# Expert weights split by ScalarE and token rows turned by VectorE in an adaLN block with mixture of experts

## The chip, the core and the metric

The kernel runs on one core of a Trainium2 chip. A core has TensorE (PE; its weight loads are shown apart as PEld), VectorE (DVE), ScalarE (ACT), GpSimd (POOL) and SyncE (SP), each with an instruction queue of its own that is worked off in order, and 16 DMA engines that they share. The metric is the device time of one execution in microseconds, as the median of several runs. The profiled execution is one of its own; its span, from the first instruction to the last, is what the profile's rows add up in.

## The reference

32 sequences of 256 tokens with 128 features each (8192 tokens) pass through one transformer block in float32. Cut to what matters:

```python
mod = (silu(c) @ wmod).reshape(32, 6, 1, 128)          # shift, scale, gate for both halves
h = layernorm(x) * (1 + ca) + sa
x = x + ga * attention(h)                              # 16 heads of 64, causal, softmax over the queries
h = layernorm(x) * (1 + cb) + sb
scores = sigmoid(h @ gate_weight.T);  sc = scores + gate_bias
# 32 experts in 4 groups of 8: the best 2 groups of a token, in them its best 6 experts
tw = scores[topidx] / (sum + 1e-20) * 0.2
routed = sum_e cw[e] * ((silu(h @ w_gate[e]) * (h @ w_up[e])) @ w_down[e])       # 64 wide each
shared = (silu(h @ sh_gate) * (h @ sh_up)) @ sh_down                             # 64 wide
anchor = the same with one of 16 pairs, 32 wide, that of the best expert         # times 0.1
x = x + gb * (routed + shared + anchor)
```

Two facts matter below. A token visits exactly two of the four groups. And the weight of an expert is a factor per token, so it can be multiplied onto the hidden activations before the down product.

## The kernel before

Tokens are handled in 16 chunks of 512 (`CH`); 128 partitions hold four tokens each (`NT` is 4). The order of the instructions on every engine is the order in which the Python code issues them (`manual_schedule`); a table of portions with due steps (`deal`) places the layer norms and the routing between the matmuls.

**Attention** (up to about 884 us) runs over 16 x 8 pairs of heads. Beside it each chunk is normalised a second time, and its rows, 128 features (`D`) followed by 4 x 13 routing numbers (`NG` groups of `GW`), are put into the tile `rows`. The features are turned by a way through DRAM: `through_dram` writes them (`hd`), `load_blocks` reads them back in four DMAs so that each 32 x 32 block lies where a VectorE stream transpose (`norm2_turn`) makes the whole matrix of it. The routing numbers of a group are its eight expert weights, the weights of its four anchor pairs, and the row of the result that the token is to be written to; `route_write` puts the weights in with GpSimd. `route_send` then scatters every row twice, once to each of its token's groups, into the DRAM tensor `rows_d`, where the tokens of one group stand together. `late_loads` loads the down weights `wd_sb` and `ad_sb` at attention step 9 (`s == NP + 1`).

**The expert part** works through 35 tiles (`LISTS`) of 512 rows of one group. Which group and which rows a tile has is computed on the chip (`Tiles`), so SP reads two words of a table per tile and uses them in addresses. A tile has five up products `k` (four of the 8 x 64 expert columns, 128 at a time, `KU` is 4, and one of the 4 x 32 anchor columns); `up(j, k)` multiplies the turned rows `h` with gate and up weights into PSUM, ScalarE applies Silu, VectorE multiplies with the up product and then with the tokens' weights `bt`. `down(j, k)` multiplies that with the down weights into `py`, and stands on TensorE behind the next `up`. `send` copies `py` and scatters the rows with four GpSimd DMAs into `y_d`, one row for each (token, group).

What a tile needs is prepared during earlier tiles, from the loop at L1403:

- `fetch_rows(j + 3)` and `fetch_weights(j + 2)` at k = 0. Rows come as one DMA of 128 partitions x 4 whole rows; gate and up weights as four.
- `weights_mine(j + 2)` at k = 1: VectorE masks the routing numbers of all four groups by the tile's own group and sums over the groups. The table `mine` for that is made in `Tiles`.
- `weights_turn(j + 2)` at k = 2: TensorE transposes the weights, ScalarE copies them out of PSUM (`cwt`), SP writes them to DRAM (`cd`) and reads them back spread over the partitions (`bt`) in six DMAs. Partition 64 q + i of product k holds expert 2 k + q's hidden unit i, so each k has weights of its own in `bt`.
- `rows_turn(j + 1)` at k = 3: four TensorE transposes of the rows, one ScalarE copy to `h`.

**The closing pass.** Once both results of all tokens of a chunk are written, from tile 17 on, `pass_load` reads them (`s`, two tiles) and the gate at k = 4. `pass_sum` at k = 3 of the next tile adds both and the shared result on VectorE and multiplies by the gate on GpSimd; `pass_out` at k = 1 of the tile after it adds the residual and stores. Between attention and the tiles stand seven pairs of the shared expert (`shared_up`, `shared_down`), beside which the first tiles are prepared.

All DMAs of this part except the scatters are issued by SP, in program order.

Of the kernel before, what the change touches and what calls it, by code (L numbers as in the profile page):

```python
# [50 lines left out]
ROW = D + NG * GW  # L51
# [5 lines left out]
def adaln_block_kernel(  # L57
# [80 lines left out]
    def late_loads():  # L138

        nc.sync.dma_start(out=wd_sb, in_=w_down.rearrange("(k p) m -> p k m", p=P))  # L140
        nc.sync.dma_start(out=ad_sb, in_=an_down.rearrange("(k p) m -> p k m", p=P))
        nc.sync.dma_start(out=sg_sb, in_=sh_gate)
        nc.sync.dma_start(out=su_sb, in_=sh_up)
        for h in range(P // SI):
            nc.sync.dma_start(out=sd_sb[h * SI : (h + 1) * SI], in_=sh_down)
# [174 lines left out]
    with ExitStack() as actx:  # L320
# [325 lines left out]
        def norm2_modulate(c):  # L646
            rows = rowp.tile([P, NT, ROW], F32, tag="rows", name=f"rows_{c}")
            modulated(rows[:, :, 0:D], chunk[c].pop("xh"), chunk[c].pop("mb2"))
            chunk[c]["rows"] = rows
# [124 lines left out]
        def route_place(c):  # L774
# [17 lines left out]
                chunk[c]["rows"][:, :, D:].rearrange("p i (g w) -> p i g w", w=GW)[:, :, :, GW - 1],  # L792
# [44 lines left out]
        def route_write(c):  # L837

            w, ws, one = (chunk[c].pop(k) for k in ("w", "ws", "one"))
            meta = chunk[c]["rows"][:, :, D:].rearrange("p i (g w) -> p i g w", w=GW)  # L840
            wk = w.rearrange("p i (g k q) -> p i g k q", g=NG, q=2)
            for q in range(2):
                nc.gpsimd.tensor_tensor(
                    meta[:, :, :, q * EPG // 2 : (q + 1) * EPG // 2], wk[:, :, :, :, q],
                    ws.unsqueeze(2).unsqueeze(3).to_broadcast([P, NT, NG, EPG // 2]), ALU.mult,
                )
# [118 lines left out]
        class Tiles:  # L965


            def __init__(self, n, segments, name):
# [4 lines left out]
                self.mine = k_([n, NG], f"{name}_mine")  # L973

            def steps(self):
# [54 lines left out]
                def g():  # L1030
                    nc.vector.tensor_copy(self.table, self.where)

                    nc.vector.tensor_tensor(
                        self.mine,
                        self.where[:, 0, :].unsqueeze(2).to_broadcast([P, n, NG]),
                        tile_no[:, 0:NG, 0].unsqueeze(1).to_broadcast([P, n, NG]),
                        ALU.is_equal,
                    )
# [109 lines left out]
        yp = actx.enter_context(tc.tile_pool(name="y", bufs=3, reuse_waits="tile"))  # L1148
        fin = actx.enter_context(tc.tile_pool(name="fin", bufs=3, reuse_waits="tile"))
# [9 lines left out]
        def fetch_rows(j):  # L1159
# [4 lines left out]
            t["rw"] = rwp.tile([P, NT, ROW], F32, tag="rw", name=f"rw_{j}")  # L1164
            got = nc.sync.dma_start(
                out=t["rw"],
                in_=rows_d[bass.ds(r, CH), :].rearrange("(p i) f -> p i f", i=NT),
            )
            if j < FIRST:
                tc.declare_no_dep(  # L1170
                    got.ins, group="late rows", reason="this tile holds rows of earlier chunks"
                )
                tc.add_to_no_dep_group("first tiles", got.ins)

        def fetch_weights(j):
            t = T[j]
            g = t.pop("g_sp")
            for key, src, srca in (("wg", w_gate, an_gate), ("wu", w_up, an_up)):
                w = wp.tile([P, KU + 1, P], F32, tag=key, name=f"{key}_{j}")
                nc.sync.dma_start(  # L1180
                    out=w[:, 0:KU, :].rearrange("p k f -> p (k f)"),
                    in_=src[:, bass.ds(g * (KU * P), KU * P)],
                )
                nc.sync.dma_start(out=w[:, KU, :], in_=srca[:, bass.ds(g * P, P)])
                t[key] = w

        def weights_mine(j):

            t = T[j]
            of, n = t["of"]  # L1190
            mm = mp.tile([P, NT, NG, GW], F32, tag="mm", name=f"mm_{j}", bufs=1)
            nc.vector.tensor_tensor(
                mm,
                t["rw"][:, :, D:].rearrange("p i (g w) -> p i g w", w=GW),
                of.mine[:, n, :].unsqueeze(1).unsqueeze(3).to_broadcast([P, NT, NG, GW]),
                ALU.mult,
            )
            m = mp.tile([P, GW, NT], F32, tag="m", name=f"m_{j}")
            nc.vector.tensor_reduce(m, mm.rearrange("p i g w -> p w i g"), AX.X, ALU.add)
            ix = mp.tile([P, NT], U32, tag="ix", name=f"iy_{j}", bufs=5)  # L1200
            nc.vector.tensor_copy(ix, m[:, GW - 1, :])
            t.update(m=m, ix=ix)

        def weights_turn(j):
            t = T[j]
            m = t.pop("m")
            pc = ps_mm.tile([(GW - 1) * NT, P], F32, tag="mm", name=f"pc_{j}")
            nc.tensor.transpose(
                pc, m[:, 0 : GW - 1, :].rearrange("p w i -> p (w i)"), ident
            )  # L1210
            cwt = mp.tile([(GW - 1) * NT, P], F32, tag="cwt", name=f"cwt_{j}", bufs=2)
            nc.scalar.copy(cwt, pc)
            cd = cwd.tile([GW - 1, CH], F32, tag="cd", name=f"cd_{j}")
            nc.sync.dma_start(out=cd.rearrange("w (i p) -> (w i) p", p=P), in_=cwt)
            bt = bcp.tile([P, KU + 1, CH], F32, tag="bt", name=f"bt_{j}")
            for q in range(2):
# [286 lines left out]
```

## Time and profile before

| | |
|---|---|
| Median of 3 runs | 1422.85 us (1421.65 to 1423.9) |
| Profiled execution, time | 1432.95 us |
| Profiled execution, span | 1431.2 us |
| Attention, from the start to the first shared product | about 884 us |
| Expert tiles, first up product to last down product | 911 to 1411 us |
| TensorE busy | 1355.9 us (95%) |
| VectorE busy | 1039.5 us (73%) |
| ScalarE busy | 796.8 us (56%) |
| GpSimd busy | 763.7 us (53%) |
| DMA packets, bytes | 183599, 182.5 MB |
| of them under 512 B | 81520 |

Busy time is the sum of an engine's instructions and says nothing of what waits for what. The costliest groups of the expert part, from the page (line, engine, operation, result and operands with shapes, count; then busy us and mean ns of one; then idle time before them and what ended most of it):

```profile
L1246 DVE TENSOR_TENSOR a<-a,pu 128x512 f32<-128x512 f32 x175 | 120.1, 686 | 149.2 <-PE pu L1243 107.1
L1245 ACT ACTIVATE a<-pg 128x512 f32<-128x512 f32 x175 | 104.5, 597 | 181.3 <-PE pg L1242 117.7
L1242 PE MATMUL pg<-h,wg 128*128 128x512 f32 x350 | 180.7, 598 | 2.1 <-ACT h L1235 2.1
L1243 PE MATMUL pu<-h,wu 128*128 128x512 f32 x350 | 179.6, 595 | 0.0
L1268 PE MATMUL py<-wd_sb,a 128*128 x1120 | 148.1, 275 | 2.3 <-DVE a L1247 2.3
```

VectorE and ScalarE mostly wait for TensorE's products; TensorE hardly waits at all. A float32 product stands there as two records, so 175 products are 350.

### The profile page before, as it was taken

What the parts mean: (1) busy time and instruction counts of PE and PEld (TensorE: products, weight loads), DVE (VectorE), ACT (ScalarE), POOL (GpSimd) and SP (SyncE); (2) the same over time, 40 slices, a digit from 0 to 9 for tenths busy, and PEclk for the clock granted to TensorE, in tenths of its full rate; (3) what the DMA queues carried; (4) which work ended last, traced back from release to release, by engine and by line L of the source; (5) the groups of instructions that cost most, each with busy time, mean ns of one, the idle gap of its engine ahead of it and who ended that gap; (6) DMA issues with size and microseconds to landing.
All of it is one profiled execution on the core that took longest, in us unless ns stands there. A gap on an engine that the chain in (4) does not pass through costs nothing. (4 is left out here: it accounts for less than half of the span.)

```text
span 1431.2 us, 33682 instructions
## 1 busy us (share of the span) xinstructions
PE 1355.9 (95%) x10543; PEld 841.2 (59%) x10543; DVE 1039.5 (73%) x4277; ACT 796.8 (56%) x2767; POOL 763.7 (53%) x1294
## 2 busy tenths in 40 slices
PE   6999999999999999999999997889999999999994
PEld 2566565565565565565565664455666666656662
DVE  5666878878878878888878775666755667766664
ACT  3777677777777776777777774322333333332331
POOL 3536467767767767767767546335232233434333
PEclk9999999999999999999999999999999999999997
DMA  4773622022022022022131013676677787888782
GB/s 151 273 264 106 217 73 59 32 74 60 31 74 60 30 73 59 32 74 54 36 73 46 30 44 104 163 205 177 172 197 194 190 221 212 241 246 244 233 211 68
DMA packets 183599, 182.50 MB, mean 128 GB/s; under 512 B 81520, under 2 KB 142656, under 8 KB 178944
## 3 DMA queue, kind: packets, MB, share of 16 engines
q1 hardware_dynamic: 172112, 159.62, 40.3%
q0 software_dynamic: 10624, 20.21, 4.2%
q8 instruction: 86, 1.41, 0.4%
q14 instruction: 89, 0.73, 0.2%
q10 hardware_dynamic: 688, 0.53, 0.1%
HBM read 121.37 MB, written 59.70 MB: 127 GB/s over the span
## 5 line engine op out<-in xcount | busy, mean ns | idle before, releaser
L549 ACT ACTIVATE e<-e,mn 128x256 f32<-128x256 f32 (+1 forms) x1024 | 453.5, 445 | 216.9 <-DVE mn L539 186.5
L539 DVE CUSTOM_DVE_ANT_0 e<-psc,mask 128x256 f32<-128x256 f32 (+1 forms) x1024 | 305.5, 345 | 5.9 <-PE pq L468 1.4
L568 POOL TENSOR_TENSOR vs<-v,rc 128x256 f32<-128x256 f32 x256 | 151.6, 613 | 239.6 <-DVE rc L557 230.8
L1279 POOL DMA_INDIRECT y_d<-y,iy x140 | 138.0, 985 | 237.0 <-ACT y L1276 204.7
L518 PEld LDWEIGHTS psc<-q,k 64*128 64x128 f32 x2048 | 166.2, 187 | 113.4 <-issue 101.6
L1246 DVE TENSOR_TENSOR a<-a,pu 128x512 f32<-128x512 f32 x175 | 120.1, 686 | 149.2 <-PE pu L1243 107.1
L1245 ACT ACTIVATE a<-pg 128x512 f32<-128x512 f32 x175 | 104.5, 597 | 181.3 <-PE pg L1242 117.7
L518 PE MATMUL psc<-q,k 64*128 64x256 f32 (+1 forms) x2048 | 202.1, 336 | 0.0
L586 PE MATMUL pav<-e,vs 128*64 128x256 f32 (+1 forms) x2048 | 195.7, 333 | 6.3 <-POOL vs L568 3.9
L549 ACT ACTIVATION_READ_ACCUMULATOR e<-e,mn 128x1 f32 x1024 | 192.9, 188 | 0.0
L1268 PEld LDWEIGHTS py<-wd_sb,a 128*128 128x128 f32 x1120 | 146.5, 191 | 71.0 <-issue 53.0
L1242 PE MATMUL pg<-h,wg 128*128 128x512 f32 x350 | 180.7, 598 | 2.1 <-ACT h L1235 2.1
L1243 PE MATMUL pu<-h,wu 128*128 128x512 f32 x350 | 179.6, 595 | 0.0
L468 PEld LDWEIGHTS po<-wo_sb,z 128*64 128x64 f32 x2048 | 121.2, 138 | 70.2 <-issue 69.7
L586 PEld LDWEIGHTS pav<-e,vs 128*64 128x64 f32 x2048 | 127.3, 137 | 59.4 <-POOL vs L568 7.0
L479 DVE TENSOR_TENSOR v<-pv,bv_sb 128x512 f32<-128x512 f32 x128 | 88.3, 690 | 89.9 <-PE pv L468 63.5
L1268 PE MATMUL py<-wd_sb,a 128*128 x1120 | 148.1, 275 | 2.3 <-DVE a L1247 2.3
L856 POOL DMA_INDIRECT rows_d<-rows,ix x128 | 130.2, 1017 | 37.2 <-issue 34.5
L468 PE MATMUL pv<-wqkv_sb,n_t 128*64 128x512 f32 x512 | 133.3, 601 | 15.8 <-DVE q L489 15.6
L489 DVE TENSOR_SCALAR q<-pq,negbq 128x512 f32<-128x512 f32 x128 | 95.9, 750 | 60.3 <-PE pq L468 58.4
L468 PE MATMUL po<-wo_sb,z 128*64 128x128 f32 x2048 | 134.1, 274 | 0.0
L468 PE MATMUL pq<-n_t,wqkv_sb 128*64 128x512 f32 x512 | 133.4, 600 | 0.7 <-ACT n_t L302 0.7
(239 smaller groups left out, 1797.5 us busy)
## 6 DMA issues: line engine op xcount, KB each, us to landing
bt<-cd SPq DMA_DIRECT2D x70, 512.0 KB
rows_d<-blank SPq DMA_DIRECT2D x69, 360.0 KB
rw<-rows_d SPq DMA_DIRECT2D x35, 360.0 KB
wg<-in_w_gate_dram SPq DMA_DIRECT2D x35, 256.0 KB
wu<-in_w_up_dram SPq DMA_DIRECT2D x35, 256.0 KB
bt<-cd SPq DMA_DIRECT2D x140, 64.0 KB
s<-y_d SPq DMA_DIRECT2D x32, 256.0 KB
mb<-mod_dram SPq DMA_DIRECT2D x31, 256.0 KB
```

The lines of the kernel that those rows point to most:

```text
L468: nc.tensor.matmul(ps[r], a[:, r], b, start=start, stop=stop)
L518: nc.tensor.matmul(pb[h][:, cols], k[r, o + kb * P : o + (kb + 1) * P], q[r, o + kb * P : o + S], start=True, stop=True,)
L539: nc.vector.tensor_tensor_reduce(e[:, cols], ps[:, cols], mask[:, cols], 1.0, 3e38, ALU.add, ALU.min, mn[:, b, kb, h : h + 1],)
L549: nc.scalar.activation(e[:, cols], e[:, cols], AF.Exp, bias=mn[:, b, kb, h : h + 1], scale=-1.0, accum_out=sm[:, b, kb, h : h + 1],)
L568: nc.gpsimd.tensor_tensor(vs[:, 2 * b : 2 * b + 2], vt[:, 2 * b : 2 * b + 2, col : col + P].rearrange("p k (h d) -> p k h d", h=2), rc[:, ...
L586: nc.tensor.matmul(pav[h * DH : (h + 1) * DH, o + kb * P : o + S], vs[:, 2 * b + kb, h, :], e[:, 0 : 2 * P] if kb == 0 else e[:, 2 * P : 3 ...
L856: sent = nc.gpsimd.indirect_dma_start(out=rows_d[:, :], out_offset=bass.IndirectOffsetOnAxis(ap=ix[:, k, i : i + 1], axis=0), in_=rows[:, ...
L1242: nc.tensor.matmul(pg, t["wg"][:, k, :], t["h"], start=True, stop=True)
L1243: nc.tensor.matmul(pu, t["wu"][:, k, :], t["h"], start=True, stop=True)
L1246: nc.vector.tensor_mul(a, a, pu)
L1268: nc.tensor.matmul(t["py"][:, i, :], a[:, i * P : (i + 1) * P], w, start=k == 0 and i == 0, stop=k == KU and i == NT - 1,)
L1279: sent = nc.gpsimd.indirect_dma_start(out=y_d[:, :], out_offset=bass.IndirectOffsetOnAxis(ap=ix[:, i : i + 1], axis=0), in_=y[:, i, :], in ...
```

## The change

Six things change together.

1. Hidden units are dealt to partitions by turns: in product k, partition 8 i + e holds unit 16 k + i of expert e. The four expert products then share one set of spread weights, and `bt` shrinks from five slices to two. The gate and up weights, loaded as before into raw tiles, are rearranged by two ScalarE copies each (`split_weights`, for the next tile at k = 2 and 3); the down weights are rearranged by their load, in 20 DMAs instead of two.
2. Rows are read twice: 16 columns (`OWN`) that start at the tile's own group's routing numbers, and the 128 features as four DMAs of `load_blocks`. A row grows from 180 to 183 numbers so that 16 columns can be read for the last group too; GpSimd clears the added ones.
3. `weights_mine` and the table `mine` go.
4. The tokens' weights and the rows are turned by VectorE stream transposes instead of TensorE. The turned weights are written to `cd` in eight DMAs and spread by two.
5. `pass_sum` moves from k = 3 of the next tile to k = 0 of the one after it, `pass_out` from k = 1 to k = 4 of that tile. The tiles `s` come from a pool of their own with six buffers instead of the four of `xin`.
6. `route_write` writes an expert group's weights with one GpSimd multiply instead of two.

```diff
+OWN = 16
+ROW = D + (NG - 1) * GW + OWN
...
     def late_loads():
-        nc.sync.dma_start(out=wd_sb, in_=w_down.rearrange("(k p) m -> p k m", p=P))
-        nc.sync.dma_start(out=ad_sb, in_=an_down.rearrange("(k p) m -> p k m", p=P))
+        for g in range(NG):
+            wd_g = w_down[g * EPG * EI : (g + 1) * EPG * EI].rearrange(
+                "(e k i) m -> k i e m", e=EPG, i=P // EPG
+            )
+            for k in range(NE // NG):
+                nc.sync.dma_start(out=wd_sb[:, g * (NE // NG) + k, :], in_=wd_g[k])
+            nc.sync.dma_start(
+                out=ad_sb[:, g, :],
+                in_=an_down[g * P : (g + 1) * P].rearrange("(l i) m -> i l m", i=LI),
+            )
...
             rows = rowp.tile([P, NT, ROW], F32, tag="rows", name=f"rows_{c}")
+            nc.gpsimd.memset(rows[:, :, D + NG * GW :], 0.0)
...
         def fetch_rows(j):
-            t["rw"] = rwp.tile([P, NT, ROW], F32, tag="rw", name=f"rw_{j}")
-            got = nc.sync.dma_start(
-                out=t["rw"],
-                in_=rows_d[bass.ds(r, CH), :].rearrange("(p i) f -> p i f", i=NT),
-            )
+            t["rw"] = rwp.tile([P, NT, OWN], F32, tag="rw", name=f"rw_{j}")
+            t["rh"] = rwp.tile([P, CH // BLK, BLK], F32, tag="rh", name=f"rh_{j}")
+            rows = rows_d[bass.ds(r, CH), :]
+            got = [
+                nc.sync.dma_start(
+                    out=t["rw"],
+                    in_=rows_d[bass.ds(r, CH), bass.ds(t["g_sp"] * GW + D, OWN)].rearrange(
+                        "(i p) f -> p i f", p=P
+                    ),
+                ),
+                *load_blocks(t["rh"], rows),
+            ]
...
+        def split_weights(j, key):
+            t = T[j]
+            raw = t[key]
+            w = wp.tile([P, KU + 1, P], F32, tag=key, name=f"{key}_{j}", bufs=2)
+            nc.scalar.copy(
+                w[:, 0:KU, :].rearrange("p k (i e) -> p k i e", e=EPG),
+                raw[:, 0 : KU * P].rearrange("p (e k i) -> p k i e", e=EPG, k=KU),
+            )
+            nc.scalar.copy(
+                w[:, KU, :].rearrange("p (i l) -> p i l", l=NG),
+                raw[:, KU * P :].rearrange("p (l i) -> p i l", l=NG),
+            )
+            t[key] = [w[:, k, :] for k in range(KU + 1)]
...
         def weights_turn(j):
-            pc = ps_mm.tile([(GW - 1) * NT, P], F32, tag="mm", name=f"pc_{j}")
-            nc.tensor.transpose(
-                pc, m[:, 0 : GW - 1, :].rearrange("p w i -> p (w i)"), ident
-            )
-            cwt = mp.tile([(GW - 1) * NT, P], F32, tag="cwt", name=f"cwt_{j}", bufs=2)
-            nc.scalar.copy(cwt, pc)
-            cd = cwd.tile([GW - 1, CH], F32, tag="cd", name=f"cd_{j}")
-            nc.sync.dma_start(out=cd.rearrange("w (i p) -> (w i) p", p=P), in_=cwt)
-            bt = bcp.tile([P, KU + 1, CH], F32, tag="bt", name=f"bt_{j}")
+            nc.vector.tensor_copy(t["ix"], rw[:, :, GW - 1])
+            m = mp.tile([P, 2, BLK], F32, tag="m", name=f"m_{j}", bufs=2)
+            nc.vector.transpose(m.rearrange("p a c -> p (a c)"), rw.rearrange("p i w -> p (i w)"))
+            cd = cwd.tile([OWN, CH], F32, tag="cd", name=f"cd_{j}")
+            to = cd.rearrange("w (a i b c) -> a b i w c", a=2, i=2, c=BLK)
+            for a in range(2):
+                for b in range(P // BLK):
+                    nc.sync.dma_start(out=to[a, b], in_=m[b * BLK : (b + 1) * BLK, a, :])
+            bt = bcp.tile([P, 2, CH], F32, tag="bt", name=f"bt_{j}")
+            for n, part in enumerate((cd[0:EPG], cd[EPG : GW - 1])):
+                of = part.shape[0]
+                nc.sync.dma_start(
+                    out=bt[:, n, :], in_=part.unsqueeze(0).to_broadcast([P // of, of, CH])
+                )
...
         def rows_turn(j):
-            ph = ps_mm.tile([P, CH], F32, tag="mm", name=f"ph_{j}")
-            for i in range(NT):
-                nc.tensor.transpose(ph[:, i * P : (i + 1) * P], rw[:, i, 0:D], ident)
             t["h"] = mp.tile([P, CH], F32, tag="h", name=f"h_{j}", bufs=2)
-            nc.scalar.copy(t["h"], ph)
+            nc.vector.transpose(t["h"], t.pop("rh").rearrange("p x r -> p (x r)"))
...
-            nc.vector.tensor_mul(a, a, t["bt"][:, k, :])
+            nc.vector.tensor_mul(a, a, t["bt"][:, k // KU, :])
...
-                if k == 1 and j + 2 < LISTS:
-                    weights_mine(j + 2)
                 if k == 2 and j + 2 < LISTS:
                     weights_turn(j + 2)
+                if k in (2, 3) and j + 1 < LISTS:
+                    split_weights(j + 1, ("wg", "wu")[k - 2])
                 if k == 3 and j + 1 < LISTS:
                     rows_turn(j + 1)
...
                     pass_load(started)
-                    due[j + 1, 3] = lambda c=started: pass_sum(c)
-                    due[j + 2, 1] = lambda c=started: pass_out(c)
+                    due[j + 2, 0] = lambda c=started: pass_sum(c)
+                    due[j + 2, 4] = lambda c=started: pass_out(c)
```

## The prediction

> **What bounds the kernel now.** I read the page's 40 slices first. The change alters nothing of weight in attention (the first 884 us), so I read the expert part: TensorE's order of work over one tile, then what SP, which issues nearly all DMAs, does in the same tile.
>
> ```profile
> PE   6999999999999999999999997889999999999994
> PEclk9999999999999999999999999999999999999997
> DMA  4773622022022022022131013676677787888782
> ```
>
> TensorE is at nine tenths or more in nearly all of the expert part, its clock granted throughout; the DMA engines are at seven to eight tenths there. TensorE's timeline in a quiet stretch:
>
> ```profile
> 1124.87 1.05 PE L1268 MATMUL py<-wd_sb,a 128*128 x8
> 1125.76 0.27 PE L1208 MATMUL pc<-ident,m 128*48 128x128 f32 x1
> 1125.87 1.02 PE L1242 MATMUL pg<-h,wg 128*128 128x512 f32 x2
> 1126.73 1.02 PE L1243 MATMUL pu<-h,wu 128*128 128x512 f32 x2
> 1127.59 1.05 PE L1268 MATMUL py<-wd_sb,a 128*128 x8
> 1128.48 0.60 PE L1233 MATMUL ph<-ident,rw 128*128 128x128 f32 x4
> 1128.92 1.02 PE L1242 MATMUL pg<-h,wg 128*128 128x512 f32 x2
> ```
>
> Matmuls overlap, so what a group costs is the step from its start to the next start: pg 0.86, pu 0.86, py 0.89, pc 0.11, ph 0.44 us. A tile is 5 x 2.61 + 0.55 = 13.6 us, and from 1038 to 1242 us the tiles follow each other at exactly 13.6 us. Later they do not: nine of them take 6.5 us more than 9 x 13.6. The timeline has the place, the last down product of a tile waiting for VectorE:
>
> ```profile
> 1256.41 1.16 PE L1268 MATMUL py<-ad_sb,a 128*128 x8 [0.52 <-DVE a L1247]
> ```
>
> VectorE was late because `pass_sum` stood ahead in its queue and waited for `s`, loaded late. Two stretches, quiet and with the closing pass (columns: us, PE, PEld, DVE, ACT, POOL, clock, DMA share, GB/s), then the queue's waits in each:
>
> ```profile
> 1005.00:1140.00 135.00, 134.54 (x650) 86.12 (x650) 84.17 (x144) 43.48 (x79) 39.45 (x40) 1.00 0.71 190
> 1215.00:1300.00 85.00, 82.31 (x390) 52.16 (x389) 58.00 (x96) 26.50 (x48) 33.00 (x35) 1.00 0.86 248
> ```
> ```profile
> SPq L1217 <- DMA cd<-cwt: 10.8, 9, 1.6
> ...
> SPq L1217 <- DMA cd<-cwt: 15.8, 5, 3.5
> ```
>
> One landing of `cd` holds SP 1.2 us in the quiet stretch and 3.2 in the busy one. SP's timeline in a quiet tile:
>
> ```profile
> 1089.81 0.42 SPq L1222 DMA_DIRECT2D bt<-cd  x1
> 1091.61 0.36 SPq L1165 DMA_DIRECT2D rw<-rows_d  x1
> 1092.49 0.36 SPq L1180 DMA_DIRECT2D wg<-in_w_gate_dram  x1
> 1093.06 0.33 SPq L1184 DMA_DIRECT2D wg<-in_an_gate_dram  x1
> 1094.42 0.33 SPq L1180 DMA_DIRECT2D wu<-in_w_up_dram  x1
> 1094.94 0.33 SPq L1184 DMA_DIRECT2D wu<-in_an_up_dram  x1
> 1099.21 0.33 SPq L1214 DMA_DIRECT2D cd<-cwt  x1
> 1101.19 1.10 SPq L1217 DMA_DIRECT2D bt<-cd  x2
> 1102.34 1.96 SPq L1222 DMA_DIRECT2D bt<-cd  x4
> ```
>
> Table words cost 1.4 us (end of 1089.81 to 1091.61), a DMA with computed address 0.53 to 0.57, one behind another 0.47 to 0.55; from 1095 to 1099 SP waits for work. So a quiet tile needs some 9.8 of 13.6 us. With the pass (two `s`, `gate`, `out`: 1.75 us, and slower landings) it needs about 15: the row fetch that SP issued 2.2 us before tile 17 began comes 6.8 us after the start of tile 23, 1.5 us lost per tile. At that lag `s` misses `pass_sum`, and TensorE stalls. **TensorE bounds, and SP stands just behind it.**
>
> **The change part by part.** Sums are made against the profiled 1431.2 us span; the execution took 1432.95, the median of the runs is 1422.85. I carry the difference over.
>
> *Turns leave TensorE.* Five transposes a tile, 0.55 us, on the bounding engine: 35 x 0.55 = 19.3. Those of the shared stage and of tiles 0 and 1, where TensorE waits for other things anyway (8.5 us idle from 900 to 960), earn nothing: about 32 tiles, **-17.6 us**.
>
> *VectorE and ScalarE.* VectorE loses L1192, L1199, L1201 (0.37 + 0.51 + 0.31 us) and gains a 128x512 stream transpose (0.70, as L456), a 128x64 one (by width about 0.2) and the cast (0.3): nothing net, hidden in the 1.2 us it idles in each 2.61. ScalarE loses `cwt` 0.26 and `h` 0.59 and gains two pairs of strided copies, 0.59 + 0.27 each by the copies of those shapes; before each up product it idles 2.0 us (a row of its timeline: `[2.01 <-PE pg L1242]`). Stride is not in the trace: between 0.86 and, doubled, 1.7 a pair; either fits. Cost 0; past 2.0 it would hold the next Silu.
>
> [...]
>
> *DMA engines.* Per tile, from the trace's packet records (mean ns a packet, over 16 engines). Removed: wide `bt`, 128 x 566 + 128 x 100, 5.3 us; rows, 128 x 119, 1.0. Added: `bt` 256 x 100, 1.6; rows as 2048 packets of 128 B at 12.7 ns (the row: `load_blocks` in attention), 1.6; own columns, 512 of 64 B at no more than that, 0.4; `cd` as 128 B, 0.2. A pass tile falls from 12.1 to 9.6 us. [...] Were a small packet as dear as one of 512 B (28 ns in these records), the additions would be 6.5 instead of 3.8, the tile 12.3 of 13.05. The row decides for its pattern; only its start addresses differ (732 B rows). I take 12.7 and keep 28 for a rival.
>
> *SP's queue,* the new burden. Per tile: words 1.4, own columns 0.6, four row blocks at 0.58 = 2.3, weights 2.1, eight `cd` writes at 0.45 (between the 0.38 of one alone and 0.53) = 3.6, landing 1.2, `bt` 1.1: **12.3 us** against TensorE's new 13.05. It fits by 0.75. With the pass: +1.75, landing half a us slower than quiet, and about 0.45 for completion counters (eight, taken in turn) = 14.5. Counted the other way, from the observed 15: -2.1 (`bt` from 3.2 to 1.1), +2.3, +3.2, less 1.5 (landing 3.2 to 1.7) and 1.3 (counters behind 512 KB transfers) = 15.6. I take **15.0**, ends 13.9 and 16.5.
>
> So from tile 17 SP falls behind: tiles 17 and 18 (no `out` yet) 1.1 each, eleven full ones 1.95 each, 0.3 for those without a load: 24; it starts 1.2 ahead (its first `cd` goes out 5.9 us into the tile, behind VectorE, and 3.6 + 1.2 + 1.1 later the next tile's words are read), and `out`, now after up product 4, makes SP wait for VectorE once, 1. Lag 23.8. What it may be: `s` is loaded 13.3 us after SP's start of the tile, lands 3.8 later, and is needed at 27.5 (2 tiles plus 1.4): 10.4. The raw weights, needed by ScalarE at 18.9, landed at 8.4: 10.5. (For the kernel before the same count gives 6.5, where it did stall.) So 23.8 - 10 = **+13.8 us** of stalls, in place of **-6.5** that go.
>
> *Later sums.* Two up products, 5.2 us, more for `s`; that is in the 10.4. The price is the end: `pass_sum` of chunk 13 now follows the last tile. Its multiply stands on POOL behind four scatters, then come its `out` add, chunk 14's two adds, its multiply and `out` add, and behind its store the loads of chunk 15. Before, POOL's multiply 14 (1417.61 to 1419.02) was followed by the add at 1419.05. Added: multiply 1.4, add 0.7, two adds 1.4, the rest hand-overs: **+4 us**.
>
> *Start.* SP needs 13 us for the first three row fetches (8.4 before, 881 to 889.4) and 10 more for `cd` and `bt`; but `hd` of chunk 15, which took 6.4 us to land behind 1.25 MB of `bt`, has less ahead. About 0, ends -2 and +4. POOL's memset and one multiply fewer (0.15 to 0.3 us a chunk) and 20 weight loads instead of two at attention step 9, where SP mostly waits (480 us in all): 0.
>
> Sum: -17.6 + 13.8 - 6.5 + 4 = **-6.3**: span about 1425, median **1416**.
>
> **Rivals.** (1) *SP never binds* (13.9 per pass tile, lag 10): -17.6 - 6.5 + 4 = -20, **1403**. For: slots of 0.38, and DMA engines far less busy. Against: the same queue lagged before with fewer issues. (2) *SP becomes the bound and overdraws*: one mechanism, the 11 added issues, at 16.2 us a full pass tile: 2 x 2.3 + 11 x 3.15 + 0.3 - 0.2 = 39.4, stalls 29.4, +9.3, **1432**, slower. It decides from 15.5 us a tile, where stalls make up the 20 won. For: 15 observed before. Against: half of that was waiting behind wide `bt`. (3) *Small packets cost as 512 B ones*: engines at 0.94, landings as slow as the 3.2 seen at 0.86, a pass tile 16: stalls 26.7, **1429**. (4) That the transposes stay on TensorE is excluded: its instruction list has none of them.
>
> **How the numbers follow.** Forecast 0.45, (1) 0.18, (2) 0.22, (3) 0.15. The forecast's own range, SP at 14.5 to 15.5, is 1410 to 1423; with the rivals 1401 to 1434. A difference under 0.2% (2.8 us) cannot be told from none: faster 0.36 + 0.18 = 0.54; same 0.08 + 0.05 = 0.13; slower 0.33.
>
> **What would show it.** Quiet tiles 13.05 us apart on TensorE; SP waiting for VectorE's turned weights before its first `cd` in them; in pass tiles SP's row fetch coming ever later, and the stalls at VectorE behind `s`, or at ScalarE behind raw weights, only from about tile 24. DMA share near 0.5 quiet and 0.65 with the pass. Two multiplies of chunk 13 after the last scatter. I am wrong if quiet tiles exceed 13.2, if ScalarE's copies exceed 2 us a pair, or if SP's `cd` slots leave 0.38 to 0.53.

## The result and the profile after

The changed kernel takes 1467.38 us (median of four runs, 1466.25 to 1468.45) beside 1422.25 us for the kernel before on the same chip: ratio 1.032, 95% interval 1.0297 to 1.0343. It is slower. The profiled execution spans 1466.6 us, 35.4 us more than that of before (1431.2; that one execution was slower than its median, so the spans differ by less than the medians do).

First the page's 40 slices of the changed kernel:

```profile
PE   6999999999999999999999987999998998788893
PEclk9999999999999999999999999899999999999997
DMA  4864532122112112213212125545454555566552
```

In the kernel before, TensorE is at nine tenths to the end of the tiles; here it has gaps in the 31st slice and from the 34th on. The DMA engines, at seven to eight tenths before, are at four to six. So TensorE waits for something other than busier DMA engines. The same two kinds of stretch, quiet and with the closing pass (columns: us, PE, PEld, DVE, ACT, POOL, granted clock, DMA share, GB/s):

```profile
1005.00:1140.00 135.00, 130.88 (x604) 81.14 (x604) 77.19 (x135) 60.47 (x100) 36.28 (x39) 1.00 0.48 123
1190.00:1395.00 205.00, 174.46 (x730) 103.43 (x731) 119.13 (x194) 73.36 (x120) 70.22 (x71) 0.94 0.59 156
```

The kernel before in the second of these stretches:

```profile
1190.00:1395.00 205.00, 200.16 (x951) 127.86 (x951) 138.00 (x225) 63.94 (x117) 79.64 (x84) 1.00 0.83 235
```

TensorE is idle 4 us in the quiet stretch already, and 31 of 205 us in the other, where it was idle 5 us before. Its tiles show it as well, each taken from the start of the last down product of the tile before to that of its own. Tiles 8 to 12 follow at 13.05 us, as predicted; then come 14.3, 15.2, 14.8, 15.1, 15.2 still without the pass, and up to 20.2 with it. What the engines waited for from 1040 to 1430 us (total us, times, longest):

```profile
ACT wg L1201 <- DMA wgr<-in_w_gate_dram: 83.3, 21, 6.7
...
PE py L1269 <- DVE a L1248: 43.2, 31, 4.0
...
DVE s L1348 <- DMA s<-y_d: 32.1, 13, 4.1
...
DVE a L1248 <- DMA bt<-cd: 16.1, 15, 2.0
```

Three different loads come late: raw weights, `s`, `bt`. They have one thing in common, the queue that issues them. Here is SP's timeline over one quiet tile, from one read of the tile's rows to the next (start, us, instruction; a row with x8 runs from the start of the first to the end of the last):

```profile
1109.49 0.41 SPq L1170 DMA_DIRECT2D rw<-rows_d  x1
1110.09 2.00 SPq L403 DMA_DIRECT2D rh<-rows_d  x4
1112.27 0.35 SPq L1190 DMA_DIRECT2D wgr<-in_w_gate_dram  x1
1112.81 0.35 SPq L1193 DMA_DIRECT2D wgr<-in_an_gate_dram  x1
1113.41 0.33 SPq L1190 DMA_DIRECT2D wur<-in_w_up_dram  x1
1113.93 0.36 SPq L1193 DMA_DIRECT2D wur<-in_an_up_dram  x1
1114.39 5.06 SPq L1224 DMA_DIRECT2D cd<-m  x8
1120.63 1.23 SPq L1228 DMA_DIRECT2D bt<-cd  x2
1123.82 0.40 SPq L1170 DMA_DIRECT2D rw<-rows_d  x1
```

From 1109.49 to 1123.82 is 14.3 us, in a tile that TensorE could do in 13.05. The queue waits only once, 1.2 us for its own writes to land before `bt` can be read, and eight writes take a third of the tile. What comes of it is in ScalarE's timeline of the same tile:

```profile
1116.93 1.08 ACT L1201 COPY wg<-wgr 128x512 f32<-128x512 f32 x1 [3.70 <-DMA wgr<-in_w_gate_dram]
1117.91 0.41 ACT L1205 COPY wg<-wgr 128x128 f32<-128x128 f32 x1
1118.23 0.59 ACT L1246 ACTIVATE a<-pg 128x512 f32<-128x512 f32 x1
1118.71 1.05 ACT L1201 COPY wu<-wur 128x512 f32<-128x512 f32 x1
```

And in TensorE's:

```profile
1114.19 1.02 PE L1244 MATMUL pg<-h,wg 128*128 128x512 f32 x2
...
1120.32 1.16 PE L1269 MATMUL py<-wd_sb,a 128*128 x8 [1.64 <-DVE a L1248]
```

ScalarE stands 3.70 us at the copy of weights that SP issued late. The Silu behind the copies starts at 1118.23, 3.0 us after its product is done (1115.21); VectorE's multiplies follow it, and TensorE loses 1.64 us at the next down product. SP's lag is the time from the last down product of the tile before to SP's table read for three tiles ahead; a negative lag means that SP is early. It grows from 1.8 us at tile 1 to 14.0 at tile 13 with no pass yet, stays at 14 to 15 while TensorE stalls, and is 16 to 19.6 with the pass. The chain that ended last puts SP's own queue at 8% of the span, where before it had 1%:

```profile
PE 11%; SPq 8%; DMA 6%; issue 4%; DVE 4%; POOL 1%; ACT 0%; POOLq 0%; DVEq 0%; ACTq 0%
```

The difference of the spans, from the starts of the tiles' last down products: 34 tile periods are 515.8 us after and 480.6 before. At each kernel's undisturbed period (13.05 and 13.6) they would be 443.7 and 462.4. So turns taken off TensorE saved 18.7, stalls rose from 18.2 to 72.1 (+53.9), the first tile ends 2.2 earlier, the end takes 23.3 instead of 20.9 (+2.4): -18.7 + 53.9 - 2.2 + 2.4 = +35.4. Of the 72.1, 9.4 fall in the first seven periods, 9.4 in the next ten and 53.3 in the rest, from tile 18 on; before, these were 13.1, 0 and 5.1.

### The profile page after: what moved, and what is told of

It is laid out like the page before. It is cut to its first block, busy times and chain, and to the rows that moved or that the text cites. A ratio compares the mean times of both kernels' runs of the same rounds, so it can differ in the third digit from the quotient of the medians.

```text
span 1466.6 us, 33979 instructions
## 1 busy us (share of the span) xinstructions
PE 1354.6 (92%) x10368; PEld 826.7 (56%) x10368; DVE 1033.0 (70%) x4275; ACT 857.8 (58%) x2837; POOL 771.3 (53%) x1294
## 5 line engine op out<-in xcount | busy, mean ns | idle before, releaser
L1280 POOL DMA_INDIRECT y_d<-y,iy x140 | 141.4, 1010 | 344.4 <-ACT y L1277 312.3
L1269 PE MATMUL py<-wd_sb,a 128*128 x1120 | 153.3, 280 | 44.1 <-DVE a L1248 43.9
L1244 PE MATMUL pg<-h,wg 128*128 128x512 f32 x350 | 187.3, 618 | 0.0
L1244 PE MATMUL pu<-h,wu 128*128 128x512 f32 x350 | 185.0, 611 | 0.0
L1248 DVE TENSOR_TENSOR a<-a,bt 128x512 f32<-128x512 f32 x175 | 124.4, 711 | 21.6 <-DMA bt<-cd 16.1
```

Of the source, the lines that this page charges most:

```text
L1244: nc.tensor.matmul(ps, t[key][k], t["h"], start=True, stop=True)
L1248: nc.vector.tensor_mul(a, a, t["bt"][:, k // KU, :])
L1269: nc.tensor.matmul(t["py"][:, i, :], a[:, i * P : (i + 1) * P], w, start=k == 0 and i == 0, stop=k == KU and i == NT - 1,)
L1280: sent = nc.gpsimd.indirect_dma_start(out=y_d[:, :], out_offset=bass.IndirectOffsetOnAxis(ap=ix[:, i : i + 1], axis=0), in_=y[:, i, :], in ...
```

## The experiments

Three theories went in. **Q**: SP's issue time bounds. **C**: ScalarE's rearranging copies hold up the Silu. **P**: small packets load the DMA engines. Each group of four ran on one chip beside the kernel before; that one took 1435.46, 1419.41 and 1434.5 us there, so only ratios are compared. Even they are rough across groups: the first seven tile periods, which the edits hardly touch, sum to 101 to 103 us in experiments 5 to 8 and to 107 to 115 us in the others. Line numbers of variants shift by a few.

**1. Half of the `cd` writes on another queue.**

```diff
-                    nc.sync.dma_start(out=to[a, b], in_=m[b * BLK : (b + 1) * BLK, a, :])
+                    (nc.sync, nc.gpsimd)[b % 2].dma_start(out=to[a, b], in_=m[b * BLK : (b + 1) * BLK, a, :])
```

> The changed kernel with four of the eight cd writes of a tile issued by GpSimd instead of SP; same data, same packets. Theory Q (SP's issue time per tile bounds the expert part: 14.9 us in a quiet tile and 16.5 to 17 in a pass tile against TensorE's 13.05): SP sheds 4 x 0.62 = 2.5 us a tile, quiet tiles come back to 13.05 us, pass tiles to about 14.3; time 1467 - 30 to 45 = 1422 to 1437. Rival C (ScalarE's copies, 1.08 + 0.41 us a pair, push back the Silu behind them): no change, 1460 to 1470. Rival P (the 2800 small packets a tile make landings late): no change, 1460 to 1470.

Measured: ratio 0.9977 (0.9965 to 0.9988). Same packets, same copies, four issues fewer on SP, and 3.4% of the time come back, some 49 us where 30 to 45 were expected. Quiet tiles are at 13.05 throughout; SP's lag stays at about 1 or less until tile 17 and reaches 15.9 with the pass. Q holds.

**2. The tokens' weights turned by TensorE again, one write.** The rows stay with VectorE, ScalarE gets a copy more.

```diff
-            m = mp.tile([P, 2, BLK], F32, tag="m", name=f"m_{j}", bufs=2)
-            nc.vector.transpose(m.rearrange("p a c -> p (a c)"), rw.rearrange("p i w -> p (i w)"))
+            pc = ps_mm.tile([NT * OWN, P], F32, tag="mm", name=f"pc_{j}")
+            nc.tensor.transpose(pc, rw.rearrange("p i w -> p (i w)"), ident)
+            cwt = mp.tile([NT * OWN, P], F32, tag="cwt", name=f"cwt_{j}", bufs=2)
+            nc.scalar.copy(cwt, pc)
...
+            nc.sync.dma_start(out=cd.rearrange("w (i p) -> i w p", p=P), in_=cwt)
```

> The changed kernel with the tokens' weights turned by one TensorE transpose and one ScalarE copy, as in the kernel before, and written to cd by one DMA instead of eight; rows are still turned by VectorE. Theory Q: SP sheds 5.4 - 0.4 = 5 us, quiet tiles 9.9 us of SP and 13.16 on TensorE, pass tiles 12.1 of SP: TensorE bounds nearly everywhere; time 1405 to 1415, under the kernel before. Rival C: ScalarE gets a copy more, 1465 to 1475. Rival P: 256 of 2800 small packets go, 1455 to 1467.

Measured: ratio 0.9894 (0.9862 to 0.9926), faster than both kernels. Quiet tiles are at 13.16 (0.11 for the one transpose), and so are most with the pass; SP's lag is about -3 in quiet tiles and at most 5.3. Its windows in the stretch with the pass:

```profile
1190.00:1395.00 205.00, 203.20 (x944) 129.13 (x942) 158.63 (x222) 96.05 (x167) 79.99 (x86) 1.00 0.65 175
```

TensorE 203.2 of 205 us busy, at a higher DMA share than the changed kernel's 0.59.

**3. ScalarE's copies left out.** The raw weights go to TensorE as they lie, so hidden units and their weights no longer match.

```diff
-            nc.scalar.copy(
-                w[:, 0:KU, :].rearrange("p k (i e) -> p k i e", e=EPG),
-                raw[:, 0 : KU * P].rearrange("p (e k i) -> p k i e", e=EPG, k=KU),
-            )
...
-            t[key] = [w[:, k, :] for k in range(KU + 1)]
+            t[key] = [raw[:, k * P : (k + 1) * P] for k in range(KU + 1)]
```

> The changed kernel without ScalarE's rearranging copies: the products read the raw weights in the order of the load, so hidden units and their weights no longer belong together. Theory Q: SP's work is the same, so tiles stay at SP's pace; only the deadline of the raw weights moves back by 5 to 8 us, which SP's lag uses up once: 1450 to 1462. Rival C: all of the loss goes, 1405 to 1420. Rival P: 1455 to 1467.

Measured: ratio 1.0415 (1.0382 to 1.0448), no faster than the change. C falls: the copies are not what bounds. Q's number was wrong too. I had expected a gain because ScalarE no longer waits for raw weights; but with SP as slow as ever the lag grows on until the next thing is late. From 1040 to 1430 us of this variant:

```profile
DVE a L1239 <- DMA bt<-cd: 35.4, 16, 4.6
...
DVE s L1339 <- DMA s<-y_d: 33.1, 13, 4.8
```

`bt` costs 35.4 where it cost 16.1, at a lag of 16 to 22 us. Why it is even slower than the changed kernel is open.

**4. The issues added to the kernel before.** Seven writes of the same shape into scratch that nobody reads; nothing else of the change.

```diff
+            cx = cwd.tile([16, CH], F32, tag="cx", name=f"cx_{j}")
+            to = cx.rearrange("w (a i b c) -> a b i w c", a=2, i=2, c=BLK)
+            for n in range(7):
+                nc.sync.dma_start(out=to[n // 4, n % 4], in_=cwt[0:BLK, 0:BLK])
```

> The kernel before with seven more DMAs a tile on SP, of the shape of the changed kernel's cd writes (32 rows of 128 B into a scratch tensor that nobody reads); nothing else changes, its computation is whole. Theory Q: 7 x 0.62 = 4.3 us more SP a tile, 14.1 quiet (over TensorE's 13.6) and 19 with the pass: 1470 to 1495. Rivals C and P: 224 small packets are 0.2 us of the DMA engines, 1420 to 1426.

Measured: ratio 1.0208 (1.0167 to 1.025). The issues alone make a slower kernel out of the old one, in direction as Q has it and well beyond C and P, but less than I had put down. The old quiet tile had about 3.8 us to spare and seven writes take some 4.5: SP's lag grows from -0.7 at tile 7 to 5.4 at tile 13 and stops there, and quiet tiles stay at 13.6. Only tiles with the pass pay (most of them 15 to 17.7 us).

**5. Rows turned by TensorE again,** by one load instead of four; the weights stay with VectorE and eight writes.

```diff
-                *load_blocks(t["rh"], rows),
+                nc.sync.dma_start(out=t["rh"], in_=rows[:, 0:D].rearrange("(i p) f -> p i f", p=P)),
...
-            nc.vector.transpose(t["h"], t.pop("rh").rearrange("p x r -> p (x r)"))
+            for i in range(NT):
+                nc.tensor.transpose(ph[:, i * P : (i + 1) * P], rh[:, i, :], ident)
+            nc.scalar.copy(t["h"], ph)
```

> The changed kernel with the rows turned by TensorE again: one load of 512 rows of 512 B in place of the four block loads, four transposes and a ScalarE copy to h. Theory Q (SP's issue time bounds): SP's quiet tile falls from 14.9 to 13.2 us (three DMAs fewer), TensorE's rises from 13.05 to 13.5; so quiet tiles stay at 13.5, SP lags only with the pass (about 15 us), and the ratio to before is 0.998 to 1.015. Rival C (ScalarE's copies): one more copy a tile, so no faster than the change, 1.03 or more. Rival P (small packets): part of them go, 1.01 to 1.02, which would not part from Q; then the lag of SP's row fetch tells.

Measured: ratio 1.0019 (1.0009 to 1.0029), in Q's range. Quiet tiles are at 13.49, lag 1.4; with the pass the lag grows to 17. Three issues fewer and 0.44 us more on TensorE are a gain of 3%, since SP was the bound.

**6. The sums at their old places.**

```diff
-                    due[j + 2, 0] = lambda c=started: pass_sum(c)
-                    due[j + 2, 4] = lambda c=started: pass_out(c)
+                    due[j + 1, 3] = lambda c=started: pass_sum(c)
+                    due[j + 2, 1] = lambda c=started: pass_out(c)
```

> The changed kernel with pass_sum and pass_out at their old places (k = 3 of the next tile, k = 1 of the one after). Theory Q: the sums wait on VectorE 5.2 us earlier for s, which SP loads late anyway, so VectorE's waits for s grow and the waits behind them (raw weights, bt) shrink by as much; the end is 2 to 3 us shorter; ratio 1.026 to 1.040. If the later place is itself a cost (the end alone), 1.028 to 1.031 with the same tile periods; if it is what keeps TensorE from worse stalls, 1.04 to 1.06.

Measured: ratio 1.033 (1.0295 to 1.0365), the change's own. SP's lag with the pass falls from 16 to 19 us to about 10, because `s` is now late before the weights are; the time is the same. The place of the sums only chooses which load is late. The end is 20.1 us.

**7. The same eight writes to flat destinations.** Experiments 1 to 6 say that SP bounds; this and 12 ask why a write costs 0.62 us there. The reading of `cd` does not follow the new order, so this variant's weighting is wrong and only its time counts.

```diff
-            to = cd.rearrange("w (a i b c) -> a b i w c", a=2, i=2, c=BLK)
+            to = cd.rearrange("w (x c) -> (w x) c", c=BLK)
...
-                    nc.sync.dma_start(out=to[a, b], in_=m[b * BLK : (b + 1) * BLK, a, :])
+                    n = (a * (P // BLK) + b) * BLK
+                    nc.sync.dma_start(out=to[n : n + BLK], in_=m[b * BLK : (b + 1) * BLK, a, :])
```

> The changed kernel with each of the eight cd writes going to one contiguous stretch of 32 x 128 B (outermost extent 32) instead of 2 x 16 x 128 B (outermost extent 2); as many writes, as many packets; the weights then stand in another order in cd, which the reading does not follow, so the weighting is left wrong. If the slot of 0.62 to 0.67 us is due to the shape of the destination: slots of 0.40 to 0.50, SP's quiet tile about 13.3, ratio 1.005 to 1.018. If it is the price of any such write behind another: slots stay at 0.62 to 0.67 and the ratio at 1.028 to 1.036.

Measured: ratio 0.9906 (0.9874 to 0.9938), below the range I had given. The step from one `cd` write to the next is 0.46 us (median) where it was 0.62, and the first table read behind `bt` takes 0.34 instead of 0.78. Quiet tiles are at 13.05, and SP waits for VectorE in them (1 us a tile).

**8. Two writes of 512-B rows.** VectorE still turns the weights, but in eight 32 x 32 pieces that come to lie side by side on 32 partitions.

```diff
-            m = mp.tile([P, 2, BLK], F32, tag="m", name=f"m_{j}", bufs=2)
-            nc.vector.transpose(m.rearrange("p a c -> p (a c)"), rw.rearrange("p i w -> p (i w)"))
+            m = mp.tile([BLK, 2, P // BLK, BLK], F32, tag="m", name=f"m_{j}", bufs=2)
+            for b in range(P // BLK):
+                for a in range(2):
+                    nc.vector.transpose(
+                        m[:, a, b, :],
+                        rw[b * BLK : (b + 1) * BLK, 2 * a : 2 * a + 2, :].rearrange("p i w -> p (i w)"),
+                    )
...
+            to = cd.rearrange("w (a i p) -> a i w p", a=2, i=2)
+            for a in range(2):
+                nc.sync.dma_start(out=to[a], in_=m[:, a].rearrange("r b c -> r (b c)"))
```

> The changed kernel with the weights turned by eight 32 x 32 VectorE transposes whose results are put side by side on 32 partitions, so that two writes of 512-B rows fill cd instead of eight of 128-B rows. Theory Q: SP's quiet tile falls from 14.9 to about 11 us and the pass tile to about 13.3; quiet tiles 13.05, pass tiles 13.05 to 13.6, SP's lag below 8 us to the end; VectorE has about 0.6 us more a tile and hides it; ratio 0.978 to 0.992. Rival C: 1.03, since ScalarE's copies are all there. Rival P: nearly all small packets (rows, own columns, bt as before) stay, so 1.02 to 1.03.

Measured: ratio 0.9944 (0.992 to 0.9968), just outside Q's range. Quiet tiles are right, SP's lag stays below 4.7, but tiles with the pass take 13.8 with no load late. The timeline of one shows something else:

```profile
1268.07 0.97 POOL L1284 DMA_INDIRECT y_d<-y,iy  x1 [0.30 <-issue]
...
1268.86 1.66 DVE L1216 CAST iy<-rw 128x4 uint32<-128x4 f32 x1
...
1269.05 1.44 POOL L1355 TENSOR_TENSOR s<-s,gate 128x256 f32<-128x256 f32 x2
...
1270.44 1.21 DVE L1220 STREAM_TRANSPOSE m<-rw 32x32 f32<-32x32 f32 x8
...
1273.14 0.38 PE L1273 MATMUL py<-wd_sb,a 128*128 x1 [0.50 <-DVE a L1252]
```

The cast of four numbers a partition takes 1.66 us and ends with GpSimd's multiply; in quiet tiles it takes 0.16. It holds VectorE, whose eight transposes follow, and TensorE waits 0.50 at its next down product. The size is that of the two in turn: 0.16 + 1.44 = 1.60. The changed kernel's trace has the same on a smaller scale: five of its 35 casts run beside the first of the two multiplies, take 0.69 us and end 0.03 us behind it; the other 30 take 0.15 to 0.17. In the tile above the cast starts 0.19 us ahead of the multiplies, while GpSimd still issues a scatter, and it is the cast that grows; why that is so, no trace here shows. Theory **G** is that the later sums put the multiply beside the cast and that this costs the 0.75 us a tile. The next two test it.

**9. The cast one product later,** behind the turn of the rows, in the kernel of experiment 8.

```diff
-            nc.vector.tensor_copy(t["ix"], rw[:, :, GW - 1])
+            t["own"] = rw
...
             nc.vector.transpose(t["h"], t.pop("rh").rearrange("p x r -> p (x r)"))
...
+            nc.vector.tensor_copy(t["ix"], t.pop("own")[:, :, GW - 1])
```

> The variant with two cd writes, and in it the cast of the row numbers (iy, four numbers a partition) moved from k = 2 to k = 3 behind the turn of the rows; nothing else. In the variant the cast takes 1.53 us in tiles with the pass and 0.16 in quiet ones, and each time GpSimd's multiply of the sums (1.44 us) runs beside it; TensorE then waits 0.5 us. Theory G (the cast waits for GpSimd, and the later sums put the multiply there): the cast is back near 0.16 to 0.4 us, pass tiles go from 13.8 to 13.05 to 13.3, ratio to before 0.986 to 0.991. If the 0.75 us a tile are SP's or the eight transposes': pass tiles stay at 13.8, ratio 0.993 to 0.996.

Measured: the cast is at 0.13 us and tiles with the pass are at 13.05 (one at 13.17) until the 28th, so without the collision the 0.75 us a tile are gone. The ratio, 0.9932 (0.9907 to 0.9957), was nevertheless not in theory G's range but in that of its rival. With TensorE faster, SP's lag grows to 13 and three of the last tiles pay 0.9 to 1.0; and the first seven periods are 112.1 us where experiment 8 had 102.4. The tile periods part the two theories, the ratio does not: from tile 18 on 2.0 us are lost to stalls, in experiment 8 9.0.

The collision alone is not the cause either. In experiment 7 the cast takes 1.61 to 1.70 us in tiles 19 to 25, and all of them are at 13.05; in experiment 2 it takes as long in most tiles with the pass, which are at 13.16. In 7 one transpose of 0.24 us follows the cast on VectorE, in 2 none, in 8 eight that take 1.21 us. So it was the collision and the eight transposes together.

**10. The sums at their old places in the kernel of experiment 8,** with the edit of experiment 6.

> The variant with two cd writes, with pass_sum and pass_out at their old places; the cast stays at k = 2. Theory G: GpSimd's multiply now runs at another time than the cast, which falls to 0.16 to 0.4 us; the end is 2 to 3 us shorter; s must be there 5.2 us earlier, which an SP lag of 4.5 us allows; ratio 0.983 to 0.989. If s comes late instead: VectorE waits for s of 1 us and more a tile, ratio 0.990 to 1.000.

Measured: the cast at 0.19 us, tiles with the pass mostly at 13.05 to 13.5, the end 20.0 us; ratio 0.9907 (0.9882 to 0.9932). The mechanism is as expected. The ratio is 0.2% above G's range and in that of the other possibility, a late `s`, but VectorE's waits for `s` from 1190 to 1410 us are 1.8 us in all and not 1 us a tile; the first seven periods are the slowest of all here, 114.6 us.

**11. The same edit in the kernel of experiment 2.**

> The variant with the tokens' weights turned by TensorE and one cd write, with pass_sum and pass_out at their old places. It had ratio 0.989, its cast 1.48 us in pass tiles, TensorE waiting 3.3 us in all. Theory G: the cast falls to 0.16 to 0.4 us, the end is 2 to 3 us shorter, ratio 0.984 to 0.989; s late would make it 0.990 or more.

Measured: ratio 0.9947 (0.9927 to 0.9967): a miss. The cast is short (0.19) and `s` is not late, but from 1190 to 1410 us VectorE waits 37.6 us for ScalarE's Silu, where experiment 2 had 6.3, and most tiles with the pass take 14 to 15. Why is open.

**12. Eight writes with another order of extents.** The columns to be turned are taken with the four row blocks innermost, so that a write goes to 8 x 4 x 32 numbers instead of 2 x 16 x 32. Same number of writes and packets; this one computes what the changed kernel computes.

```diff
-            nc.vector.transpose(m.rearrange("p a c -> p (a c)"), rw.rearrange("p i w -> p (i w)"))
+            nc.vector.transpose(m.rearrange("p a c -> p (a c)"), rw.rearrange("p i w -> p w i"))
...
-            to = cd.rearrange("w (a i b c) -> a b i w c", a=2, i=2, c=BLK)
+            to = cd.rearrange("(a w) (i b c) -> a b w i c", a=2, i=NT, c=BLK)
```

> The changed kernel, eight writes of 32 rows of 128 B each, with expert and row block swapped in the order of the columns that are turned, so that the destination of a write has extents 8 x 4 x 32 numbers instead of 2 x 16 x 32; same packets, same addresses overall. If the slot of 0.62 us comes from the outermost extent of 2: slots of 0.45 to 0.50 and a ratio of 0.985 to 0.996, like the flat destination (0.9906). If it comes from a destination of three extents rather than two: slots of 0.60 to 0.67, ratio 1.028 to 1.036.

Measured: ratio 1.0012 (0.9997 to 1.0026), a little above the range for the outermost extent and far from the other. SP's timeline:

```profile
1125.37 3.58 SPq L1226 DMA_DIRECT2D cd<-m  x8
1129.12 1.46 SPq L1230 DMA_DIRECT2D bt<-cd  x2
1132.08 0.41 SPq L1170 DMA_DIRECT2D rw<-rows_d  x1
```

Eight writes in 3.58 us instead of 5.06: (3.58 - 0.33) / 7 = 0.46 a step, and 1.50 us for the words (1130.58 to 1132.08) instead of 1.96. So three extents are not what is dear; 2 x 16 is. Two lines take 3% off the changed kernel. That it does not reach experiment 7's 0.99 goes with SP's 15.1 us in a tile with the pass (14.6 there): from tile 18 on 18.5 us are lost to stalls, there 8.1.

SP's parts of a tile, from its instruction list, start of each to start of the next, waits for VectorE left out, means over seven or eight quiet tiles:

| us a tile | predicted | changed | exp. 7 | exp. 12 |
|---|---|---|---|---|
| table words | 1.4 | 1.67 | 1.26 | 1.22 |
| own columns | 0.6 | 0.75 | 0.70 | 0.74 |
| four row blocks | 2.3 | 2.21 | 2.38 | 2.35 |
| weights | 2.1 | 2.46 | 2.50 | 3.30 |
| eight `cd` writes | 3.6 | 5.40 | 3.82 | 3.77 |
| landing of `cd` | 1.2 | 1.02 | 0.17 | 0.47 |
| `bt` | 1.1 | 1.27 | 1.24 | 1.35 |
| sum | 12.3 | 14.8 | 12.1 | 13.2 |
| with the pass, period of SP | 15.0 | 17.0 | 14.6 | 15.1 |

The 5.40 is a mean; in five of the eight tiles the writes took 5.14 to 5.17. Experiment 12's 3.30 for the weights holds gaps between issues that no wait in the trace explains; its SP still keeps up with TensorE in quiet tiles (lag about 0).

## Why the prediction was wrong

The mechanism is the one that was named, SP's queue, and it was the second rival that came, in a larger size: SP is the bound and overdraws. The step that failed is a term of the sum for SP's queue: "eight `cd` writes at 0.45 (between the 0.38 of one alone and 0.53) = 3.6". They take 5.40, 1.8 of the 2.5 us by which SP's tile was undercounted. I priced the writes by rows of other shapes, one write with a flat destination and loads; the new shape, whose outermost extent is 2, was in no row. With that the first table read behind it grew too (words 1.67 for 1.4). So the quiet tile is 14.8 instead of 12.3 us, **above TensorE's 13.05 instead of below it**, and the lag that was to begin at tile 17 begins at the start. "It fits by 0.75" was a margin smaller than the uncertainty of eight slots, and the range should have said so: 0.09 us more a slot uses it up, and the slots came out 0.17 (median) to 0.22 us dearer. I had bounded the slot from above by a row, 0.53, that had no right to be a bound.

Put the slot near where I had it and the forecast nearly comes out. Experiment 7, with slots of 0.46, has 12.1 quiet and 14.6 with the pass, and ratio 0.9906; predicted were 12.3, 15.0 and 1416 / 1422.85 = 0.995. Experiment 12, the same correction with the result unchanged, has 1.0012; the forecast's own range, 1410 to 1423, is 0.991 to 1.000. So one lies just below the range and one just above it, and the slots account for 3.1 to 4.1% where forecast and result are 3.7% apart.

Point by point:

- *Turns leave TensorE*, -17.6: right. Tiles that nothing disturbs take 13.05 us, -18.7 over 34 periods.
- *VectorE*, net nothing: right in size (0.70, 0.24, and 0.16 for the cast, put at 0.3). Left out was where the cast and GpSimd's multiply stand relative to each other after the later sums. In the changed kernel TensorE's stalls mostly kept them apart (the cast averages 0.32 from 1190 to 1395 us). With fewer stalls they meet; by experiments 2 and 7 VectorE's idle time hides it with the change's one transpose, by 8 and 9 not with eight.
- *ScalarE's copies*, 0.86 a pair, doubled 1.7: 1.06 to 1.08 and 0.41, so 1.49; within both ends and under the 2.0 that would matter. Hidden: in experiment 2 they run in every tile, and tiles are at 13.16.
- *DMA engines*: right. In the quiet stretch of the changed kernel (1005 to 1140 us) a 128-B packet takes 13.8 ns, a 64-B one 11.2 and a 512-B one 29.2; shares are 0.48 and 0.59 for 0.5 and 0.65. The third rival is out.
- *What the lag may be*, 10 us: plateaus at 14 to 15 in quiet tiles, 4 us more than counted. That error was in the change's favour.
- *SP with the pass*: the first count adds up to 15.0 (12.3 + 1.75 + 0.5 + 0.45), not to the 14.5 written there. The 15.0 that was carried on is not touched by it; experiments 7 and 12 have 14.6 and 15.1.
- *Stalls*, +13.8 in place of -6.5, so +7.3: measured +53.9. Nearly all of it goes with the slots: from tile 8 on the changed kernel loses 62.7 us, with slots of 0.46 it is 8.1 (experiment 7) and 18.5 (experiment 12), on either side of the 13.8.
- *Later sums*, +4 at the end: +2.4. They bring nothing while SP bounds (experiment 6).
- *Turns on VectorE rather than on TensorE*: on the ground of who has time, the choice was right; in the quiet stretch of before VectorE was busy 84.17 of 135 us and TensorE 134.54. But experiments 2 and 5 show what the other choice saves: the 32 x 32 blocks are paid for in DMA issues (eight `cd` writes for one, four loads of rows for one) rather than in packets, and SP had no time for them. The variant with the lowest ratio (experiment 2, 0.9894) turns the weights on TensorE and the rows on VectorE.

## What to carry to other kernels

Where one queue issues nearly all DMAs, count its time per stage like that of an engine, per instruction, and price an issue by a row with the same access pattern on both sides; a new pattern is an unknown with an open upper end, however small the data. If a block layout needs many small writes, look first for another order of the columns (here 8 x 4 instead of 2 x 16 outside the rows), or for a turn that puts several blocks side by side, as well as for giving work back to another engine, which had the lowest ratio here. And after a queue has been relieved, look again at which instructions now meet: here a cast beside GpSimd's multiply grew from 0.16 to 1.66 us, and together with eight transposes behind it that cost 0.75 us of a 13.05 us tile, which nothing had shown while SP was slower.

## What the hardware showed that was not expected

*The price of these issues depended on the shape of the destination.* With 32 rows of 128 B each, one behind another on SP: 0.62 us (0.66 in experiment 1; means 0.64 to 0.68) for 2 x 16 x 32, 0.46 for 8 x 4 x 32 and for a flat 32 x 32; in the kernel before, among the other work of experiment 4, 0.62 again. No trace here shows why. The middle extent (16 and 4) changes along with the outer one (2 and 8), so which of the two is the cause is open. That it is not the number of extents is shown: 2 x 16 x 32 and 8 x 4 x 32 have three each.

*A table read behind such DMAs was dear:* 0.78 us instead of 0.33 (the kernel before), in the changed kernel and in experiments 1, 2, 5 and 8, which all write `cd` with an outermost extent of 2 or 4; 0.34 and 0.35 in 7 and 12; 0.52 in experiment 4, where six reads of `bt` stand between.

*TensorE ran at about half speed for a while at six of its long stalls.* The changed kernel, TensorE's timeline:

```profile
1219.08 1.02 PE L1244 MATMUL pu<-h,wu 128*128 128x512 f32 x2
1223.89 2.07 PE L1269 MATMUL py<-wd_sb,a 128*128 x8 [3.79 <-DVE a L1248]
1225.76 1.92 PE L1244 MATMUL pg<-h,wg 128*128 128x512 f32 x2
1227.46 1.79 PE L1244 MATMUL pu<-h,wu 128*128 128x512 f32 x2
1229.09 1.05 PE L1269 MATMUL py<-wd_sb,a 128*128 x8
```

After 3.79 us of waiting, three groups take 1.8 to 2.1 us instead of 1.0, together 2.6 us lost by their starts (5.20 from 1223.89 to 1229.09 against 2.61). The granted clock of that time (columns as above):

```profile
1222.20:1229.00 6.80, 5.11 (x12) 3.22 (x13) 3.11 (x7) 2.67 (x4) 1.86 (x2) 0.50 0.46 113
```

From 960 us to the last tile the clock record has 0.5 in six stretches, five of 3.4 us and this one of 6.8, each beginning during a wait of 2.1 to 4.0 us or at most 1.2 us behind it; after two more waits, of 2.5 and 2.7 us, and after those of 1.5 to 1.7 it stays at 1.00. So the length of the wait alone does not decide: one of 2.1 us was followed by a drop, one of 2.7 was not, and what does decide is not shown. In the stretch with the pass the clock is 0.94 with the stalls and 1.00 in experiments 2, 9 and 10 without them. TensorE was busy 22 us at half clock, so by estimate at most 11 of the 53.9 us can have come of it; less where SP was later still.
